# Four graph layers on one core: edge scores taken two slots in a pass, with copies moved between engines and loads respaced

## The chip, the core and the metric

The kernel runs on one core of a Trainium2 chip. The metric is the device time of one execution in microseconds, from the first to the last instruction with what the launch puts around it. The engines are named as in the profile: PE multiplies matrices, DVE is the vector engine, ACT the scalar engine, POOL is GpSimd, which here does nothing but issue indirect (gathering and scattering) DMAs and a few plain ones, and SP issues most of the plain DMAs.

## What is computed

`x` is 16 batches of 1024 nodes with 256 features, `adj` a 1024 x 1024 matrix in which few elements of a row are not zero. All is float32.

```python
# layer 0
pre_u = h @ W1[:d];  pre_v = h @ W1[d:]
hidden = relu(pre_u[:, :, None, :] + pre_v[:, None, :, :] + b1)
S = sigmoid(hidden @ W2 + b2)                       # one score for each pair u, v
a = einsum('buv,bud->bvd', S * adj, h)
m = einsum('uv,bud->bvd', adj, h) * h
z = beta1*h + beta2*(a @ Wa + ba) + beta3*(m @ Wm + bm)
# layer 1
z = z + relu((adj @ z) @ W.T + b)
# layers 2 and 3, with weights of their own
f = z @ W1.T;  f1 = f @ W2 + b2
c = softmax(leaky_relu(f1[:, None] + f1[None, :]) + adj)
z = c @ f + bias2 + z
```

The scores S are needed only where `adj` is not zero, and that is how the kernel takes them.

## The kernel before

**Stages.** Rows of a node are laid on 128 partitions, so there are NT = 8 node tiles. The 16 batches are worked in NGR = 4 groups of GB = 4.

1. *Start* (lines 363 to 505): `load_h` (275) brings the batches of the first group, `load_w1` (151) the weights W1 and Wa. `first_group` turns the features with PE (`turned`) and makes both sides of the edge sum (`edge_sides`, 305), which go to memory as `u_d` and `v_d`. DVE meanwhile finds the non-zero elements of each row of `adj`: up to SLOTS = 32, of which FIRST = 16 belong to the node itself and the others go to XT = 6 tiles of extra rows with QUAD = 4 slots.
2. *First part* (909 to 959): `score_free` does what needs no scores, for all 16 batches: `messages` (332, the product with `adj`), `without_edges` (347), `turned` and `edge_sides` of later groups.
3. *Four groups*, one after another (1302 to 1316). `with_edges` (1058) multiplies the scores of the group, read back from memory (`load_gd`) and reordered by ACT (`gc`, line 1066), with `hw`. Then `pair_layers` (1198) takes two batches at a time through `layer_one` (1134) and the two attention layers: `front` (971) makes the features `f`, `scales` (990) the exponentials `rho` and `tau`, and `sums` (1029) forms for each of 8 node tiles a product `m` on DVE (line 1038) and multiplies it by `f` on PE.

**The scores.** `score_steps` (706) is a generator that runs beside stages 2 and 3, one slot of one node tile in a step, for four batches at once: 128 x 1024 elements. A step gathers the rows of `v_d` for a later slot (`fetch`, 859, by POOL), adds the row of `u` to the gathered rows (807, DVE), takes relu and the product with W2 (809, DVE), and sums each batch's 256 elements with four activations that accumulate (813, ACT). After the last slot of a tile the gates are formed (822 to 829), and their scatters into `dense` are put on a list `waiting`, from which every step issues one or two (788, POOL). A step fetches LEAD = 4 slots ahead, into LEAD + 2 buffers.

**What sets the order.** The order on each engine is fixed when the kernel is built. `Side.along` (869) runs the stage's own generator, which yields its estimated time in us, and takes so many steps of the scores for each of them:

```python
            for us in main:
                self.owed += us * rate
                while self.owed >= 1:
                    self.owed -= 1
                    next(self.steps, None)
```

The rates are RATE = (0.26, 0.255) steps per us. The tool that orders the instructions may put a later instruction of an engine ahead of one that it expects to have to wait. `product` (125) records every matrix product, and `paced` (118) makes an instruction wait for the product that lies `back` = 6 before the latest recorded one, so that side work does not run ahead of PE. One call of `product` becomes two PE instructions.

**Buffers and waits to know.** `sums` has four buffers `m`; `with_edges` has two buffers `gc` and four `gd`; PSUM has eight banks. In `front`, `evacuate` (133) copies a bank by ACT and DVE in turn (lines 138 and 136). `scales` starts `rho` with two DVE instructions out of PSUM (1013). In `with_edges` of the first group, `z_loads` brings four tiles `z` of 1 MB from `zb_d` (at node tiles 2 to 5, line 1073), and then `to_load` brings the transposed `adj` in eight loads, each followed later by an exponential (1076 to 1082). All these, `gd` among them, are issued by SP in order. For the last group there are no scores left: there the third and fourth batch take their neighbours for FAR = 6 node tiles from the lists (`by_lists`, 1139, beside `pair_layers` of the first two batches), which gathers one row of `y_d` at a time, four ahead.

## Time and profile before

| | |
|---|---|
| three timed runs | 3244.6 us median (3230.55 to 3249.76) |
| the profiled execution | 3257.53 us, of it span 3255.8 us |
| granted PE clock, mean | 0.988 |
| busy: PE / DVE / ACT / POOL | 3132.2 / 2433.7 / 1880.1 / 1826.6 us |
| line 807 (DVE, add), line 809 (DVE, relu and product) | 608 of each, 1220 ns each |
| line 813 (ACT, sums) | 2432, 405 ns each, and 188 ns to read the sum |
| line 697 (POOL, gathers of `v_d`) | 512 + 96, 1279 and 1331 ns |
| line 702 (POOL, scatters into `dense`) | 512 + 96, 1238 and 1156 ns |
| lines 136, 138 (copies of features) | 128 at 418 ns (DVE), 128 at 375 ns (ACT) |
| line 1013 (first pass of `rho`) | 64 at 742 ns (DVE) |

A group's mean duration counts from an instruction's start to its end. Instructions of one engine overlap at their edges, so the distance from start to start is shorter: PE's products with 257 columns last 384 ns each in the groups, but 64 of them in a row take 14.0 us. A window of the trace is given as its start and end in us from the start of the span; beside each engine's busy time it lists the number of instructions (x), then the granted PE clock, the share of the DMA engines' time and GB/s. "x <- y" in the waits says that x's engine stood idle until y released it.

### The profile page before, as it was taken

How to read it: one execution, taken by the hardware profiler on the slowest of the kernel's cores; microseconds unless marked ns; L12 is line 12 of the kernel's file. 1: busy time of each engine (PE TensorE's matmuls, PEld its weight loads, DVE VectorE, ACT ScalarE, POOL GpSimd, SP SyncE). 2: the span in 40 equal slices, each digit the busy share in tenths (PEclk: the TensorE clock that was granted, in tenths of full speed). 3: DMA queues.
4: the chain of work that ended last, by engine and by line, in shares of the span. 5: the costliest groups of instructions: out<-in, count | busy, mean ns of one | idle time of the engine just before them, and what ended most of it. 6: DMA issues, size and time to landing. Idle time of an engine off the chain costs nothing. (4 is left out here: it accounts for less than half of the span.)

```text
span 3255.8 us, 39220 instructions
## 1 busy us (share of the span) xinstructions
PE 3132.2 (96%) x12122; PEld 2203.5 (68%) x12122; DVE 2433.7 (75%) x3366; ACT 1880.1 (58%) x6320; POOL 1826.6 (56%) x1483
## 2 busy tenths in 40 slices
PE   8999999999997999999999999999999999999999
PEld 5544544555556678578776867778686678858888
DVE  7787777777775799799668979867898872148754
ACT  3245556566667766566976656688666654413232
POOL 1146888676664666657566666665676550066600
PEclk9999999999998999999999999999999999999999
DMA  8998898879799755656875575587656525475600
GB/s 286 328 323 305 278 288 267 272 226 275 240 322 317 214 162 162 205 154 209 291 226 174 151 221 154 182 286 232 182 151 210 169 90 168 127 246 142 167 15 27
DMA packets 281899, 687.49 MB, mean 211 GB/s; under 512 B 45184, under 2 KB 137344, under 8 KB 274512
## 3 DMA queue, kind: packets, MB, share of 16 engines
q0 software_dynamic: 128224, 387.80, 41.0%
q1 hardware_dynamic: 125472, 245.45, 22.0%
q10 hardware_dynamic: 27984, 51.65, 4.2%
q8 instruction: 97, 1.59, 0.2%
q14 instruction: 122, 1.00, 0.1%
HBM read 553.45 MB, written 131.32 MB: 210 GB/s over the span
## 5 line engine op out<-in xcount | busy, mean ns | idle before, releaser
L813 ACT ACTIVATE z<-z 128x256 f32<-128x256 f32 x2432 | 978.9, 405 | 702.6 <-DVE z L809 613.4
L807 DVE TENSOR_TENSOR z<-z,u 128x1024 f32<-128x1024 f32 x608 | 739.2, 1220 | 402.9 <-PE bank L126 263.0
L126 PE MATMUL bank<-feats,m 128*128 128x257 f32 x4096 | 926.1, 384 | 30.5 <-DVE m L1038 21.7
L697 POOL DMA_INDIRECT z<-v_d,slot_v x512 | 655.1, 1279 | 471.2 <-ACT z L813 241.6
L126 PEld LDWEIGHTS bank<-feats,m 128*128 128x128 f32 x4096 | 768.4, 191 | 160.1 <-DVE m L1038 28.2
L702 POOL DMA_INDIRECT dense_d<-gt,slot_at x512 | 634.1, 1238 | 198.7 <-issue 139.6
L809 DVE SCALAR_TENSOR_TENSOR z<-z,w2r 128x1024 f32<-128x1024 f32 x608 | 737.9, 1220 | 8.5
L126 PE MATMUL bank<-gc,hw 128*128 128x256 f32 x2048 | 459.3, 385 | 33.1 <-ACT gc L1066 28.4
L126 PEld LDWEIGHTS bank<-gc,hw 128*128 128x128 f32 x2048 | 388.4, 192 | 103.4 <-ACT gc L1066 40.5
L813 ACT ACTIVATION_READ_ACCUMULATOR z<-z 128x1 f32 x2432 | 458.2, 188 | 0.0
L126 PE MATMUL bank<-adj_sb,h 128*128 128x512 f32 x1024 | 442.5, 592 | 2.8 <-ACT st L323 2.6
L1038 DVE SCALAR_TENSOR_TENSOR m<-rho,tau,adj_sb 128x512 f32<-128x512 f32 x512 | 374.3, 744 | 69.7 <-PE bank L126 66.2
L126 PE MATMUL bank<-adjT_in,y 128*128 128x512 f32 (+1 forms) x960 | 401.5, 579 | 5.1 <-DMA adjT_in<-adjT_d 2.6
L126 PEld LDWEIGHTS bank<-adj_sb,h 128*128 128x128 f32 x1024 | 194.3, 190 | 243.1 <-issue 237.7
L126 PE MATMUL bank<-w,hT 128*128 128x512 f32 (+1 forms) x1024 | 337.9, 490 | 10.8 <-DMA w<-in_L_gnn_W_dram 8.7
L126 PEld LDWEIGHTS bank<-adjT_in,y 128*128 128x128 f32 x960 | 181.8, 190 | 220.4 <-issue 207.6
L1066 ACT ACTIVATE gc<-gd 128x1024 f32<-128x1024 f32 x128 | 264.6, 2067 | 92.1 <-PE bank L126 53.9
L126 PEld LDWEIGHTS bank<-w,hT 128*128 128x128 f32 x1024 | 195.7, 192 | 154.8 <-issue 131.5
L126 PE MATMUL bank<-g_wT,z 128*128 128x257 f32 x1024 | 235.9, 385 | 1.1 <-DVE z L1117 0.9
L697 POOL DMA_INDIRECT z<-v_d,x_node x96 | 127.7, 1331 | 175.9 <-ACT z L813 108.1
L126 PEld LDWEIGHTS bank<-g_wT,z 128*128 128x128 f32 x1024 | 194.5, 193 | 32.4 <-issue 3.3
L697 POOL DMA_INDIRECT z<-y_d,slot_v x96 | 107.4, 1119 | 62.5 <-DVE msg L1176 41.7
(162 smaller groups left out, 2385.9 us busy)
## 6 DMA issues: line engine op xcount, KB each, us to landing
gd<-dense_d SPq DMA_DIRECT2D x128, 512.0 KB
dense_d<-zero ACTq DMA_DIRECT2D x64, 512.0 KB
adjT_in<-adjT_d SPq DMA_DIRECT2D x112, 256.0 KB
h<-in_x_dram SPq DMA_DIRECT2D x19, 1024.0 KB
u_d<-st SPq DMA_DIRECT2D x64, 256.0 KB
v_d<-st SPq DMA_DIRECT2D x64, 256.0 KB
hw_d<-st SPq DMA_DIRECT2D x64, 256.0 KB
u<-u_d POOLq DMA_DIRECT2D x32, 512.0 KB
```

What stands on the lines that cost most here:

```text
L126: recent.append(nc.tensor.matmul(*args, **kw))
L697: return nc.gpsimd.indirect_dma_start(out=dst, out_offset=None, in_=src[:], in_offset=bass.IndirectOffsetOnAxis(ap=at, axis=0), **how,)
L702: return nc.gpsimd.indirect_dma_start(out=dst[:], out_offset=bass.IndirectOffsetOnAxis(ap=at, axis=0), in_=src, in_offset=None,)
L807: paced(nc.vector.tensor_tensor(z, z, u, ALU.add))
L809: nc.vector.scalar_tensor_tensor(zk, zk, 0.0, w2r[:, None, :].to_broadcast([P, GB, D]), ALU.max, ALU.mult)
L813: nc.scalar.activation(zk[:, c, :], zk[:, c, :], AF.Copy, accum_out=s[:, k, c : c + 1])
L1038: nc.vector.scalar_tensor_tensor(m, r[:, cols], ta[:, jt : jt + 1], ea[:, jt, cols], ALU.max, ALU.mult)
L1066: paced(nc.scalar.activation(gc, gd.rearrange("p n i -> p i n"), AF.Copy), 16)
```

## The change

A step of the scores now takes two slots. The gathered tile is 128 x 2 x 1024 elements, filled by two gathers; line 807 and line 809 each work on all 2048 elements in one instruction (the row of `u` is read twice); the ACT sums stay one for each batch and slot, eight in a step. There are three buffers of two slots, fetched two steps ahead, where there were six of one slot, fetched four ahead. What counts steps is halved: RATE, HOLD, LEAD, the steps of the searches and of the extra rows. A step issues two or three waiting scatters instead of one or two.

Beside that: `front` copies all features by ACT; the first pass of `rho` is an ACT relu with a bias; `by_lists` gathers four rows into one of the same buffers, two buffers ahead; at the start W1 is loaded ahead of the features, whose four pieces all go by SP's queue. In `with_edges` the loads of `z` are spread over every second node tile, with a pace of 12 products, the loads of the transposed `adj` begin with the second quarter (`v` = 1) and their exponentials with the third, and in the first quarter of the first group a node tile counts 1 us and not 3.4 for the rate of the scores. The diff, with some context cut:

```diff
@@ -17,7 +17,7 @@
 BUFS = 2
-RATE = (0.26, 0.255)
+RATE = (0.13, 0.1275)
 SLOTS = 32
@@ -25,9 +25,9 @@
 XT = 6
-HOLD = 40
+HOLD = 20
 FAR = 6
-LEAD = 4
+LEAD = 2
 TOP = 16.0
@@ -272,12 +272,11 @@
-    def load_h(pool, b, pieces=1, other=nc.sync):
+    def load_h(pool, b, pieces=1):
         h = pool.tile([P, NT, D], F32, tag="wide", name="h")
...
         for t in range(0, NT, n):
-            queue = other if t // n % 2 else nc.sync
-            queue.dma_start(h[:, t : t + n, :], x[b, t * P : (t + n) * P].rearrange("(t p) d -> p t d", p=P))
+            nc.sync.dma_start(h[:, t : t + n, :], x[b, t * P : (t + n) * P].rearrange("(t p) d -> p t d", p=P))
         return h
@@ -375,10 +374,9 @@
-        hs = [load_h(early, 0, pieces=4, other=nc.scalar)]
         w1 = load_w1(prep1, nc.scalar)
+        hs = [load_h(early, b, pieces=1 if b else 4) for b in range(2)]
         with_beta2(w1)
-        hs.append(load_h(early, 1))
         for t in range(NT):
@@ -683,7 +681,7 @@
             zs = stack.enter_context(tc.tile_pool(name="zs", bufs=2))
-            slot_pool = stack.enter_context(tc.tile_pool(name="slots", bufs=LEAD + 2))
+            slot_pool = stack.enter_context(tc.tile_pool(name="slots", bufs=LEAD + 1))
             wide_z = stack.enter_context(tc.tile_pool(name="wide_z", bufs=4))
@@ -711,7 +709,7 @@
                 last_of = {g: t for g, t in tiles}
-                todo = [(g, t, k) for g, t in tiles for k in range(FIRST if t < NT else QUAD)]
+                todo = [(g, t, k) for g, t in tiles for k in range(0, FIRST if t < NT else QUAD, 2)]
                 us, zt, ss = {}, {}, {}
@@ -751,7 +749,8 @@
                             fetch(us, zt, *step)
-                    yield
+                    if t % 2:
+                        yield
                 places(own)
@@ -785,18 +784,19 @@
                         last = fetch(us, zt, *todo[n + LEAD])
-                    for _ in range(0 if n < HOLD else 2 if n % 2 and len(waiting) > 4 else 1):
+                    for _ in range(0 if n < HOLD else 3 if len(waiting) > 4 else 2):
                         if waiting:
...
                             after(tc, ins, [last], later, "behind the gather")
-                    if moving:
-                        group, *what = moving.pop(0)
-                        ins = scatter(*what)
-                        group.add(ins)
-                        after(tc, ins, [last], later, "behind the gather")
-                        arrive = n + 12
+                    for _ in range(2):
+                        if moving:
+                            group, *what = moving.pop(0)
+                            ins = scatter(*what)
+                            group.add(ins)
+                            after(tc, ins, [last], later, "behind the gather")
+                            arrive = n + 6
                     slots, _, at, av = lists(t)
@@ -804,20 +804,23 @@
                         sources(us, *follows[g, t])
-                    paced(nc.vector.tensor_tensor(z, z, u, ALU.add))
-                    zk = z.rearrange("p (c k) -> p c k", k=D)
+                    u2 = u[:, None, :].to_broadcast([P, 2, GB * D])
+                    paced(nc.vector.tensor_tensor(z, z, u2, ALU.add))
+                    zk = z.rearrange("p s (c k) -> p (s c) k", k=D)
                     nc.vector.scalar_tensor_tensor(
-                        zk, zk, 0.0, w2r[:, None, :].to_broadcast([P, GB, D]), ALU.max, ALU.mult
-                    )
-                    for c in range(GB):
-                        nc.scalar.activation(zk[:, c, :], zk[:, c, :], AF.Copy, accum_out=s[:, k, c : c + 1])
+                        zk, zk, 0.0, w2r[:, None, :].to_broadcast([P, 2 * GB, D]), ALU.max, ALU.mult
+                    )
+                    for c in range(2 * GB):
+                        nc.scalar.activation(
+                            zk[:, c, :], zk[:, c, :], AF.Copy, accum_out=s[:, k + c // GB, c % GB : c % GB + 1]
+                        )
                     if n < NT:
...
                         places(others)
-                    if n == NT + 4:
+                    if n == NT + 2:
                         moved = to_extra_rows()
-                    if k == slots - 1:
+                    if k == slots - 2:
                         sv = s[:, :slots, :].rearrange("p s c -> p (s c)")
@@ -836,7 +839,7 @@
                         got = from_extra_rows(moved)
-                    if got is not None and n == arrive + 24:
+                    if got is not None and n == arrive + 12:
                         unpack(got)
@@ -857,8 +860,10 @@
             def fetch(us, zt, g, t, k):
-                z = zt[g, t, k] = slot_pool.tile([P, GB * D], F32, tag="z", name="z")
-                return gather(z, v_d[g], lists(t)[1][:, k : k + 1])
+                z = zt[g, t, k] = slot_pool.tile([P, 2, GB * D], F32, tag="z", name="z")
+                for i in range(2):
+                    last = gather(z[:, i, :], v_d[g], lists(t)[1][:, k + i : k + i + 1])
+                return last
@@ -979,7 +984,7 @@
                         )
-                    evacuate(f[:, jt, :], ps[:, : D + 1])
+                    nc.scalar.activation(f[:, jt, :], ps[:, : D + 1], AF.Copy)
                     if jt == 1:
@@ -1010,7 +1015,7 @@
                 for v in range(NV):
-                    nc.vector.tensor_scalar(r[:, v * HN : (v + 1) * HN], banks[v], sh[:, 3:4], 0.0, ALU.add, ALU.max)
+                    nc.scalar.activation(r[:, v * HN : (v + 1) * HN], banks[v], AF.Relu, bias=sh[:, 3:4])
                 nc.vector.tensor_scalar(sh[:, 1:2], sh[:, 0:1], -0.01, None, ALU.mult)
@@ -1070,17 +1075,17 @@
                                 )
-                        if z_loads and ut > 1:
+                        if z_loads and ut % 2 == 0:
                             load, i = z_loads.pop(0)
-                            paced(load(i))
-                        if (to_load or to_exp) and ut % 2 and not z_loads:
-                            if v and to_exp:
+                            paced(load(i), 12)
+                        if (to_load or to_exp) and ut % 2 and v:
+                            if v > 1 and to_exp:
                                 exponential(to_exp.pop(0))
...
                                 to_exp.append(jt)
-                        yield 3.4
+                        yield 3.4 if g or v else 1
                     if v == N // QN - 1:
@@ -1151,34 +1156,40 @@
                 todo += [(t, FIRST + q) for t in range(FAR) for q in range(NG)]
-                got = {}
-
-                def fetch_row(t, k):
-                    z = got[t, k] = slot_pool.tile([P, GB * D], F32, tag="z", name="z")[:, : 2 * D]
-                    if t < NT and k >= FIRST:
-                        at = (k - FIRST) * NT + t
-                        gather(z, part_d, to_u[:, at : at + 1])
-                    else:
-                        gather(z, y_d, lists(t)[1][:, k : k + 1])
-
-                for step in todo[:LEAD]:
-                    fetch_row(*step)
-                for n, (t, k) in enumerate(todo):
-                    if n + LEAD < len(todo):
-                        fetch_row(*todo[n + LEAD])
-                    z = got.pop((t, k))
-                    to = msg[t] if t < NT else part[t % len(part)]
-                    if t < NT and k >= FIRST:
-                        paced(nc.vector.tensor_tensor(to, to, z, ALU.add))
-                    elif k == 0:
-                        paced(nc.vector.tensor_scalar(to, z, lists(t)[3][:, k : k + 1], None, ALU.mult))
-                    else:
-                        paced(nc.vector.scalar_tensor_tensor(
-                            to, z, lists(t)[3][:, k : k + 1], to, ALU.mult, ALU.add
-                        ))
-                    if t >= NT and k == QUAD - 1:
-                        nc.sync.dma_start(part_d[(t - NT) * P : (t - NT + 1) * P, :], to)
-                    yield
+
+                fours = [todo[i : i + 4] for i in range(0, len(todo), 4)]
+                got = []
+
+                def fetch_rows(some):
+                    z = slot_pool.tile([P, 2, GB * D], F32, tag="z", name="z").rearrange("p a (b n) -> p (a b) n", b=2)
+                    for i, (t, k) in enumerate(some):
+                        if t < NT and k >= FIRST:
+                            at = (k - FIRST) * NT + t
+                            gather(z[:, i, :], part_d, to_u[:, at : at + 1])
+                        else:
+                            gather(z[:, i, :], y_d, lists(t)[1][:, k : k + 1])
+                    got.append(z)
+
+                for some in fours[:LEAD]:
+                    fetch_rows(some)
+                for n, some in enumerate(fours):
+                    if n + LEAD < len(fours):
+                        fetch_rows(fours[n + LEAD])
+                    zs4 = got.pop(0)
+                    for i, (t, k) in enumerate(some):
+                        z = zs4[:, i, :]
+                        to = msg[t] if t < NT else part[t % len(part)]
+                        if t < NT and k >= FIRST:
+                            paced(nc.vector.tensor_tensor(to, to, z, ALU.add))
+                        elif k == 0:
+                            paced(nc.vector.tensor_scalar(to, z, lists(t)[3][:, k : k + 1], None, ALU.mult))
+                        else:
+                            paced(nc.vector.scalar_tensor_tensor(
+                                to, z, lists(t)[3][:, k : k + 1], to, ALU.mult, ALU.add
+                            ))
+                        if t >= NT and k == QUAD - 1:
+                            nc.sync.dma_start(part_d[(t - NT) * P : (t - NT + 1) * P, :], to)
+                        yield
```

## The prediction

> **What bounds the kernel.** I read the page, then windows of 100 us, the groups by shape, the waits and the timeline of the stretches that stood out.
>
> ```profile
> PE 3132.2 (96%) x12122; PEld 2203.5 (68%) x12122; DVE 2433.7 (75%) x3366; ACT 1880.1 (58%) x6320; POOL 1826.6 (56%) x1483
> ```
>
> PE is the bound, and all that can be won is what it stands idle: 3255.8 - 3132.2 = 124 us, and some of the 1.2% of clock that idling costs. Where, the windows tell (busy PE, PEld, DVE, ACT, POOL):
>
> ```profile
> 400.00:500.00 100.00, 98.33 (x275) 48.93 (x274) 72.05 (x75) 54.95 (x234) 80.81 (x66) 1.00 0.88 282
> 900.00:1000.00 100.00, 85.19 (x264) 51.78 (x263) 56.90 (x59) 60.01 (x201) 59.76 (x50) 0.91 0.91 323
> 1200.00:1300.00 100.00, 97.00 (x469) 82.63 (x468) 98.61 (x150) 66.59 (x250) 61.69 (x46) 1.00 0.57 162
> 1157.00:1501.00 344.00, 331.91 (x1442) 256.60 (x1441) 310.58 (x452) 219.79 (x834) 220.03 (x168) 1.00 0.58 168
> 1734.00:2101.00 367.00, 353.68 (x1537) 274.54 (x1537) 331.97 (x485) 237.92 (x895) 230.25 (x175) 0.99 0.58 169
> 2311.00:2698.00 387.00, 370.89 (x1605) 288.63 (x1604) 331.69 (x493) 235.27 (x874) 232.75 (x178) 0.99 0.53 157
> ```
>
> In the first part (400) PE is full, with POOL the next: 80.8 us in 66 issues, and as an issue follows the last by 0.30, it has no idle time at all (80.8 + 66 x 0.30 = 100.6). Between first part and groups (900) PE loses 15 us and clock. In the three attention stretches PE is idle 41.6 us of 1098 and DVE busy 974; there DVE is the second bound, as the timeline shows:
>
> ```profile
> 1242.27 0.75 DVE L1038 SCALAR_TENSOR_TENSOR m<-rho,tau,adj_sb 128x512 f32<-128x512 f32 x1
> 1242.93 1.22 DVE L807 TENSOR_TENSOR z<-z,u 128x1024 f32<-128x1024 f32 x1
> 1244.07 0.75 DVE L1038 SCALAR_TENSOR_TENSOR m<-rho,tau,adj_sb 128x512 f32<-128x512 f32 x1
> ```
>
> Start to start, m takes 0.66 and a pass 1.14, 1.80 together, with no gap, where PE needs 8 x 0.217 = 1.74 for one m. So a DVE that has less to do lets PE run.
>
> **The change, part by part.** The sum is made in the profiled execution, 3257.5 us, and set off from the median of the runs, 3244.6, which is 12.9 lower.
>
> ```profile
> L807 DVE TENSOR_TENSOR z<-z,u 128x1024 f32<-128x1024 f32 x608 | 739.2, 1220 | 402.9 <-PE bank L126 263.0
> L136 DVE COPY feats<-bank 128x257 f32<-128x257 f32 x128 | 53.0, 418 | 12.8 <-PE bank L126 11.9 <-issue 0.5
> L138 ACT ACTIVATE feats<-bank 128x257 f32<-128x257 f32 x128 | 46.5, 375 | 61.2 <-PE bank L126 54.4 <-issue 4.7 <-PE bank L1004 1.8
> L1013 DVE TENSOR_SCALAR rho<-bank,shift 128x512 f32<-128x512 f32 x64 | 44.9, 742 | 0.0
> L1116 ACT ACTIVATE r<-bank,l1b 128x512 f32<-128x512 f32 x60 | 38.3, 678 | 71.2 <-PE bank L126 39.8 <-DVE msg L1176 26.4 <-DMA out_dram<-st 4.9
> ```
>
> 1. *DVE's relief in attention: -36.* A two-slot pass: the 512-wide addition of line 1117 takes 686, the 1024-wide 1220, so 1.043 ns an element; 2048 take 2.29 us, 2.20 in a stream, for two of 1.14. The 249 slots of the three stretches save 249 x 0.07 = 17 us. Three of four groups have scores: 96 copies (0.34 in a stream) and 48 passes of rho (0.66) leave DVE, 32 + 32. Together 81 of 974 us. DVE is over 90% busy in 6 of the 11 windows of 100 us, so 44 count; PE's idle time caps it at 41.6; I take off 5 for ACT, whose sums now come as eight in a row (8 x 0.40 = 3.2 us, not 1.6) ahead of what ends a `sums`. ACT gains 96 x 0.375 + 48 x 0.68 = 69 us in stretches where it is busy 693 of 1098, so the moved work is covered. Bounds: -41.6; and +70, if m runs out: a pass starts at the earliest when PE has five products left, 5 x 0.43 = 2.17 us, and the next m is there after 2.20 + 0.74 = 2.94; 0.77 in each of some 91 pairs that fall into `sums`. Four buffers of m, three of them ready (5.2 us), speak against that.
>
> The page "ScalarE: Activation LUTs", Rules for kernel authors, says to give relu, add and copies to VectorE, since it is up to about 3 times faster; that is for bf16. If it held here, ACT would get 3 x 64 x 0.742 = 142 us for rho. The rows above say 678 against 742 ns, and 375 against 418, and they decide.
>
> 2. *POOL beside longer passes: +15.* What a POOL issue takes depends on DVE:
>
> ```profile
> 1560.94 1.23 DVE L809 SCALAR_TENSOR_TENSOR z<-z,w2r 128x1024 f32<-128x1024 f32 x1
> 1561.62 1.40 POOL L697 DMA_INDIRECT z<-v_d,slot_v  x1 [2.10 <-ACT z L813]
> 1568.34 1.23 DVE L807 TENSOR_TENSOR z<-z,u 128x1024 f32<-128x1024 f32 x1 [1.10 <-PE bank L126]
> 1568.53 1.89 POOL L697 DMA_INDIRECT z<-v_d,slot_v  x1 [0.30 <-issue]
> ```
>
> Both issues end 0.85 after the pass beside which they started (1562.17 + 0.85 = 1563.02; 1569.57 + 0.85 = 1570.42); alone one takes 0.97, 1.27 with its gap. So an issue waits for the pass to end. In 350 to 550 POOL is full: 66 x 0.97 = 64.0 of 80.8 us, so 16.8 us per 100 are such waits, for some 53 passes. If an issue starts at an even chance in a pass of 1.14 this would be 53 x 0.89 x (0.57 - 0.12) = 21; the trace has 0.8 of it. A pass of 2.20 always catches one, in its first 1.27 us: (2.20 - 0.64 - 0.12) x 0.8 = 1.15, 26 times in 100 us, 30 us. That is +13 per 100 us for 250 full us, 33. A late gather first eats the time in which line 807 waits for its pace (71 us from 200 to 950, so 24 in this third): +9 is left, +15 with the burst of extra rows, which now falls later, onto the first scatters (20 to 26 steps in). Queued behind a late gather: line 807, then on DVE mT and zb, for which PE waits in `without_edges`. Bounds: 0 if what an issue waits for does not grow with the pass (no pass of the trace is longer than 1.23 us); +60 if three full windows lose 20 each and nothing is eaten. I take the side near the line that the two issues lie on.
>
> The page "SBUF — State Buffer", Who interferes with whom, says that a DVE instruction with two SBUF inputs holds a port shared with GpSimd for the whole instruction; by it an issue in a longer pass waits to its end (+15); if the port were given back inside one, it would not (0). This rule speaks against longer passes.
>
> 3. *Between the parts: -16.*
>
> ```profile
> PE bank L126 <- ACT gc L1066: 19.0, 8, 14.3
> ACT gc L1066 <- DMA gd<-dense_d: 13.0, 2, 12.8
> ```
>
> These are the waits of 930 to 1100. SP issues four z of 1 MB from 964.9 to 976.5, and the gd behind them lets PE stand for 14.3 us. Now one z goes out every second node tile (6.9 us), and the eight loads of adj come later, eight tiles further. Of the 19.0 I take the 14.3 and 2 of the rest. The eight exponentials (8.3 us of ACT) move one quarter on and cost there what they cost now. Bounds: 0 to -19.
>
> 4. *gc beside eight sums: +8.* A node tile of `with_edges` is 16 x 0.216 = 3.45 us of PE and 2.07 of ACT. Two tiles with one pair: 2 x 2.07 + 3.2 = 7.34 for 6.9, so 0.44 and more for each of 36 pairs, 16; the present waits of this kind outside part 3 are 28.4 - 19.0 = 9.4, so +7, +8 as some bursts lie worse. Bounds -9 and +56 (a burst that starts just before gc: 1.8 each).
>
> 5. *Start: -6.*
>
> ```profile
> PE bank L126 <- DMA w<-in_L_gnn_W_dram: 8.7, 1, 8.7
> ```
>
> W1 is now issued first. Bounds: -9.3 (with 0.6 for Wa); +4.5, the time PE waits for h now, if h takes twice as long on one queue.
>
> 6. *End of the scores: +3.* The first quarter gives (3.4 - 1) x 8 x 0.1275 = 2.4 pairs less; the scores end some 19 us later. Now the last scatter is issued at 2683.9 and PE starts on that group at 2717.7; landing, gd and gc need some 12. Bounds 0 and +15.
>
> 7. *Lists: -6.*
>
> ```profile
> 3095.50 1.09 PE L1193 MATMUL bank<-ident,msg 128*128 128x128 f32 x4 [5.48 <-issue]
> ```
>
> PE stood 3.5 and 5.5 us for the last rows, which POOL issued one each 1.26 us; with 8 to 12 rows ahead and not 4 to 6, four or five are there already. Bounds -10, +2. Halved counters, searches and pool size cost nothing; DVE's searches are the same.
>
> Sum: -36 + 15 - 16 + 8 - 6 + 3 - 6 = -38, so 3219.5 for the profiled execution and **3207** against the median.
>
> **Rivals.** *Slower: POOL becomes the bound.* Per pair POOL needs 4.1 issues x 1.27 = 5.2, 0.5 behind the m's, and twice the wait for a pass. A pair lasts 1098 / 125 = 8.78 us in attention, 8.46 with part 1; it decides from (8.46 - 5.7) / 2 = 1.38 a wait. I have 1.15, and 1.44 without the factor 0.8, so it is near. At 1.65 a pair takes 9.0: +28 there; (26 x 1.65 - 16.8) x 2.5 - 24 = +41 in the first part; the other parts -17: 3297. For it: POOL without idle time in the first part. Against: 21% idle in attention. *Slower: m runs out*, part 1 at +70: 3313. *DVE's time is not on the path:* part 1 at 0 and part 3 at half: 3251. For it: PE is busy 97% there already. *Faster:* nothing held longer, all idle time won: -42 + 0 - 19 - 9 - 9 + 0 - 10 = -89: 3156.
>
> **How the numbers follow.** Forecast 0.38 (its own range 3180 to 3235, three quarters of it below 3212); faster rival 0.18; not on the path 0.19; POOL 0.18; m runs out 0.07. About 1% is what a measurement of this kernel can tell from no change. Faster: 0.28 + 0.18 = 0.46; same: 0.10 + 0.19 = 0.29; slower 0.25. The range 3150 to 3300 leaves out half of POOL's case, m's, and a little below: 0.19.
>
> **What would show it.** Right: L807 near 2290 ns x304; DVE below 94% in 1200 to 1300; no wait of 10 us for gc near 980. POOL's issues near 1.6 us mean and line 807 waiting longer on "DMA z<-v_d" confirm part 2; over 1.7, with PE idle from 350 to 700, POOL's rival. Idle PE with "DVE m L1038" growing from 21.7 us shows m running out. The sum is wrong if attention's 41.6 us do not shrink.

## The result, and the profile after

The changed kernel takes 3481.5 us (median of 6 runs, 3477.5 to 3487.7) against 3242.7 of the kernel before (6 runs): ratio 1.0749, 95% interval 1.0727 to 1.0770. It is slower by 239 us where 38 less were predicted. Its profiled execution took 3487.7 us, span 3486.0. Kernels' times below are medians, and one execution of e9, at 6677 us twice as long as the other three, is left out of its row. "Before" and "after" name the kernel before and the changed one, a pair is the two slots of a step, and the weight pass is line 809 (810 after), relu and product with `w2`.

The page's line of engines, after:

```profile
PE 3198.5 (92%) x12122; PEld 2231.4 (64%) x12122; DVE 2295.1 (66%) x2566; ACT 1930.6 (55%) x6512; POOL 2199.8 (63%) x1483
```

DVE was relieved as planned, 2433.7 to 2295.1. POOL went the other way with the same 1483 instructions, 1826.6 to 2199.8: 373 us more. PE's span grew by 230, of which 66 are PE being "busy" longer with the same 12122 products (more on this at the end) and 164 are idle.

Windows of the kernel before (first fence) and after (second): the middle of the first part and three stretches of attention in which both have the same products (PE's counts agree within 4), and after also one window. Columns as in the prediction: PE, PEld, DVE, ACT, POOL, clock, DMA share, GB/s.

```profile
300.00:850.00 550.00, 546.71 (x1538) 278.04 (x1537) 411.19 (x435) 325.17 (x1358) 415.32 (x334) 1.00 0.84 263
...
1179.00:1555.00 376.00, 361.74 (x1601) 284.59 (x1600) 340.23 (x499) 241.99 (x909) 239.51 (x181) 1.00 0.61 178
1757.00:2132.00 375.00, 361.65 (x1596) 284.09 (x1596) 342.17 (x502) 241.78 (x907) 239.28 (x179) 0.99 0.60 175
2341.00:2717.00 376.00, 361.79 (x1593) 286.71 (x1594) 315.08 (x475) 223.55 (x818) 222.20 (x169) 0.99 0.52 152
```

```profile
300.00:850.00 550.00, 485.45 (x1292) 241.99 (x1291) 328.67 (x241) 268.54 (x1130) 456.05 (x302) 0.93 0.73 226
...
1200.00:1300.00 100.00, 93.78 (x303) 57.17 (x302) 65.06 (x58) 61.53 (x242) 75.56 (x50) 0.97 0.57 169
...
1293.00:1700.00 407.00, 371.28 (x1600) 291.45 (x1601) 315.27 (x367) 251.23 (x950) 280.24 (x181) 0.96 0.54 165
1919.00:2322.00 403.00, 366.43 (x1598) 289.07 (x1599) 319.50 (x374) 252.80 (x949) 296.22 (x185) 0.97 0.55 169
2543.00:2934.00 391.00, 367.52 (x1589) 290.70 (x1589) 304.50 (x367) 237.61 (x898) 283.84 (x178) 0.97 0.50 153
```

With its gaps of 0.30, POOL has 456.05 + 302 x 0.30 = 547 of 550 us in the first part: full for all of it. Before it had 415.32 + 334 x 0.30 = 516, so 34 us to spare, and PE stood for 3.3; now PE stands for 64.6. In attention no engine is full: DVE 78% where it had 89, POOL 72% without its gaps (62 before), and PE idles 95.8 us of 1201 where it had 41.8 of 1127.

Groups of the changed kernel (engine, operation, busy, mean ns | idle before, and what ended it):

```profile
L808 DVE TENSOR_TENSOR z<-z,u 128x2048 f32<-128x2048 f32 x304 | 696.2, 2290 | 660.9 <-DMA z<-v_d,slot_v 300.5
L695 POOL DMA_INDIRECT z<-v_d,slot_v x512 | 846.4, 1653 | 395.4 <-ACT z L814 230.8
L700 POOL DMA_INDIRECT dense_d<-gt,slot_at x512 | 751.0, 1467 | 179.3 <-issue 148.3
```

The addition takes the 2290 ns that were forecast. Gathers went from 1279 to 1653 ns, scatters from 1238 to 1467; over all 1216 issues of gathers of `v_d` and scatters the mean is 1.558 us, forecast "near 1.6" (before 1.256). The waits of after, for the lines of before (total us, times, longest):

```profile
DVE z L808 <- DMA z<-v_d,slot_v: 300.5, 73, 15.4
DVE z L808 <- PE bank L126: 225.1, 89, 19.5
...
PE bank L126 <- DVE m L1043: 53.5, 18, 14.2
...
PE bank L126 <- ACT gc L1071: 45.0, 37, 6.1
...
PE bank L126 <- ACT st L322: 40.5, 10, 8.7
...
PE bank L126 <- DVE mT L342: 38.3, 10, 14.6
```

Before, DVE waited 63.9 us for gathers, 31 times; now 300.5. What stands behind the waiting addition in DVE's queue can be late with it, and these waits grew: PE's for `m` (21.7 before) and `mT` (4.5), and for ACT's `st` (2.6) and `gc` (28.4). One such wait in the timeline of after:

```profile
421.00 2.29 DVE L810 SCALAR_TENSOR_TENSOR z<-z,w2r 128x2048 f32<-128x2048 f32 x1
421.58 2.56 POOL L695 DMA_INDIRECT z<-v_d,slot_v  x1 [0.30 <-issue]
424.44 0.96 POOL L695 DMA_INDIRECT z<-v_d,slot_v  x1 [0.30 <-issue]
425.70 1.01 POOL L700 DMA_INDIRECT dense_d<-gt,slot_at  x1 [0.30 <-issue]
...
431.45 2.29 DVE L808 TENSOR_TENSOR z<-z,u 128x2048 f32<-128x2048 f32 x1 [8.16 <-DMA z<-v_d,slot_v]
```

The first gather of a pair is held by the weight pass until 424.14, 0.85 after that pass (421.00 + 2.29). The second follows at once and takes 0.96, as DVE is idle; its rows are there 6.05 us after it ends, and DVE has stood for 8.16 us. In the groups POOL is not full, but its scatters can come in a row ahead of the gather that DVE needs next:

```profile
1529.61 0.97 POOL L700 DMA_INDIRECT dense_d<-gt,slot_at  x1 [0.31 <-issue]
...
1549.30 0.97 POOL L700 DMA_INDIRECT dense_d<-gt,slot_at  x1 [0.30 <-issue]
1550.57 0.98 POOL L695 DMA_INDIRECT z<-v_d,slot_v  x1 [0.30 <-issue]
...
1557.20 2.29 DVE L808 TENSOR_TENSOR z<-z,u 128x2048 f32<-128x2048 f32 x1 [13.48 <-DMA z<-v_d,slot_v]
```

From 1529.61 to 1550.27 it issues thirteen scatters and nothing else.

### The profile page after: what moved, and what is told of

It reads as the page before. It is cut to its first block, busy times and chain, and to the rows that moved or that the text cites. A ratio compares the mean times of both kernels' runs of the same rounds, so it can differ in the third digit from the quotient of the medians.

```text
span 3486.0 us, 38260 instructions
## 1 busy us (share of the span) xinstructions
PE 3198.5 (92%) x12122; PEld 2231.4 (64%) x12122; DVE 2295.1 (66%) x2566; ACT 1930.6 (55%) x6512; POOL 2199.8 (63%) x1483
## 5 line engine op out<-in xcount | busy, mean ns | idle before, releaser
L808 DVE TENSOR_TENSOR z<-z,u 128x2048 f32<-128x2048 f32 x304 | 696.2, 2290 | 660.9 <-DMA z<-v_d,slot_v 300.5
L695 POOL DMA_INDIRECT z<-v_d,slot_v x512 | 846.4, 1653 | 395.4 <-ACT z L814 230.8
L126 PE MATMUL bank<-feats,m 128*128 128x257 f32 x4096 | 933.6, 386 | 61.5 <-DVE m L1043 53.5
L126 PEld LDWEIGHTS bank<-feats,m 128*128 128x128 f32 x4096 | 777.7, 193 | 184.3 <-DVE m L1043 42.1
L700 POOL DMA_INDIRECT dense_d<-gt,slot_at x512 | 751.0, 1467 | 179.3 <-issue 148.3
L810 DVE SCALAR_TENSOR_TENSOR z<-z,w2r 128x2048 f32<-128x2048 f32 x304 | 695.0, 2286 | 5.0
L126 PE MATMUL bank<-adj_sb,h 128*128 128x512 f32 x1024 | 451.3, 602 | 22.5 <-ACT st L322 22.5
L126 PE MATMUL bank<-w,hT 128*128 128x512 f32 (+1 forms) x1024 | 349.6, 502 | 25.4 <-ACT st L322 18.0
L1071 ACT ACTIVATE gc<-gd 128x1024 f32<-128x1024 f32 x128 | 261.9, 2064 | 121.5 <-PE bank L126 72.1
L126 PE MATMUL bank<-g_wT,z 128*128 128x257 f32 x1024 | 247.5, 397 | 23.1 <-DVE z L1122 14.9
L695 POOL DMA_INDIRECT z<-v_d,x_node x96 | 152.9, 1593 | 140.8 <-ACT z L814 104.3
L700 POOL DMA_INDIRECT dense_d<-gt,x_at x96 | 144.5, 1505 | 29.3 <-issue 28.0
```

The source lines that it names most:

```text
L126: recent.append(nc.tensor.matmul(*args, **kw))
L695: return nc.gpsimd.indirect_dma_start(out=dst, out_offset=None, in_=src[:], in_offset=bass.IndirectOffsetOnAxis(ap=at, axis=0), **how,)
L700: return nc.gpsimd.indirect_dma_start(out=dst[:], out_offset=bass.IndirectOffsetOnAxis(ap=at, axis=0), in_=src, in_offset=None,)
L808: paced(nc.vector.tensor_tensor(z, z, u2, ALU.add))
L810: nc.vector.scalar_tensor_tensor(zk, zk, 0.0, w2r[:, None, :].to_broadcast([P, 2 * GB, D]), ALU.max, ALU.mult)
L1071: paced(nc.scalar.activation(gc, gd.rearrange("p n i -> p i n"), AF.Copy), 16)
```

## The experiments

The runs are e1 to e20, without an e4 and an e14. Runs on one chip share a letter: A has e1, e2, e3, e6; B has e5, e7, e8, e9, e13, e15, e16; C has e10, e11, e12; D has e17 to e20. One kernel's ratio differed by 1% between two chips (e16 and e20), so differences are taken on one chip where there are such. The kernel before took 3240.7 on A, 3243.8 and 3244.4 on B, 3227.3 on C and 3226.2 on D; e6, e7, e8 and e10 have two executions each. "First part" is the time at which `with_edges` first starts, then follow the lengths of the three groups with scores and of the rest, all from the traces (the profiled execution of before was 15 us above its median, that of after 6); "issue" is the mean of POOL's 1216 gathers of `v_d` and scatters into `dense`.

| kernel | us | ratio to before, 95% | issue us | first part, groups, rest |
|---|---|---|---|---|
| before | 3242.7 | | 1.256 | 956, 593, 584, 585, 538 |
| after | 3481.5 | 1.0727 to 1.0770 | 1.558 | 1064, 632, 626, 620, 544 |
| e1 passes cut (A) | 3741.5 | 1.1539 to 1.1609 | 1.167 | 1177, 667, 685, 657, 543 |
| e2 pairs only (A) | 3497.1 | 1.0777 to 1.0832 | 1.550 | 1068, 643, 625, 621, 544 |
| e3 other edits only (A) | 3225.4 | 0.9939 to 0.9972 | 1.243 | 953, 580, 578, 573, 540 |
| e6 half the scatters (A) | 3342.7 | 1.0291 to 1.0370 | 1.606 (of 912) | 998, 606, 601, 593, 549 |
| e5 cut, in order (B) | 3349.6 | 1.0291 to 1.0362 | 1.370 | 983, 610, 599, 602, 544 |
| e7 fourth buffer (B) | 3468.2 | 1.0622 to 1.0743 | 1.549 | 1045, 627, 624, 615, 543 |
| e8 w2 in PSUM (B) | 3422.5 | 1.0498 to 1.0585 | 1.473 | 1006, 628, 625, 615, 549 |
| e9 e3, four buffers (B) | 3294.5 | 1.0114 to 1.0202 | 1.252 | 985, 609, 577, 576, 546 |
| e13 slot by slot (B) | 3317.9 | 1.0186 to 1.0251 | 1.219 | 982, 603, 599, 585, 546 |
| e15 late sums (B) | 3319.5 | 1.0196 to 1.0259 | 1.197 | 989, 603, 599, 588, 542 |
| e16 e11 + fours (B) | 3251.9 | 1.0013 to 1.0044 | 1.217 | 977, 579, 578, 582, 541 |
| e10 e5 + fourth (C) | 3327.5 | 1.0280 to 1.0332 | 1.373 | 985, 609, 601, 597, 534 |
| e12 e5, six single (C) | 3324.0 | 1.0278 to 1.0322 | 1.362 | 989, 606, 602, 592, 530 |
| e11 e3 + w2 in PSUM (C) | 3206.7 | 0.9915 to 0.9948 | 1.218 | 952, 574, 574, 567, 538 |
| e17 e13, single rows (D) | 3253.5 | 1.0057 to 1.0097 | 1.206 | 970, 580, 588, 579, 536 |
| e18 e3, pair steps (D) | 3312.8 | 1.0251 to 1.0286 | 1.349 | 972, 603, 601, 589, 537 |
| e19 e11 again (D) | 3208.3 | 0.9932 to 0.9961 | 1.215 | 952, 574, 574, 569, 537 |
| e20 e16 again (D) | 3202.4 | 0.9908 to 0.9938 | 1.218 | 952, 579, 574, 568, 530 |

In the expectations "ring" means the buffers that the gathers fill in turn, and "coarse steps" that the work of two slots is handed over at once, half as often.

**Which edits? e2 and e3.** e3 is the kernel before with these edits of the change, and nothing of the pairs:

```diff
-                    evacuate(f[:, jt, :], ps[:, : D + 1])
+                    nc.scalar.activation(f[:, jt, :], ps[:, : D + 1], AF.Copy)
-                    nc.vector.tensor_scalar(r[:, v * HN : (v + 1) * HN], banks[v], sh[:, 3:4], 0.0, ALU.add, ALU.max)
+                    nc.scalar.activation(r[:, v * HN : (v + 1) * HN], banks[v], AF.Relu, bias=sh[:, 3:4])
...
-                        if z_loads and ut > 1:
+                        if z_loads and ut % 2 == 0:
```

> Kernel before (one slot in a pass, six buffers), with only the edits beside the passes: copies of features and rho's first pass on ScalarE, the part change spread, W1 ahead of the features of the graphs. Theory: these are not what was lost, and a part of the predicted relief is seen: 3190 to 3235. Rival, the edits beside the scores cost the time: over 3300.

e2 is the other half, the changed kernel with these edits undone.

> Changed kernel, with the edits beside the passes taken back: copies of features alternate between VectorE and ScalarE, rho's first pass is on VectorE, the part change loads and the start are as before. Theory, the length of the pass: the loss stays, and what the edits beside it may bring is lost too, 3480 to 3540. Rival, the edits beside the scores cost the time: about 3245.

Measured on one chip, before 3240.7: e3 -15 us, e2 +256. Together +241, and the change has +239: the pairs of slots cost it all, and the other edits gain a little, by the traces in the groups.

**GpSimd? e6.** Half of the scores stay out of `dense`:

```diff
-                        for j in range(slots):
+                        for j in range(0, slots, 2):
```

> Changed kernel that leaves out every second scatter of scores, so half of the scores never reach the dense matrix; passes, gathers, buffers and sums stay. Theory, GpSimd is the bound in the first part and late in bursts after it: with a quarter of its issues gone the gathers come in time, 3330 or less, and line 808 waits for its gathers well under 300 us. Rival, the coarse steps or the eight sums in a row: 3450 or more, since nothing there changes. If it is GpSimd and only the length of the pass lies behind it, this and the cut passes both win.

3342.7, 12.7 above what the theory gave, but 139 below the change, and 154 below e2 on the same chip (some 15 of it are the other edits, which e2 lacks). Of the 154 the first part has 70 and the three groups 89; the rest is 5 longer. Passes, gathers and buffers are those of the change; only POOL, and the DMA queue behind it, have less to do, and DVE's wait for gathers falls from 300.5 us to this:

```profile
DVE z L808 <- DMA z<-v_d,slot_v: 129.8, 45, 10.2
```

**The length of the pass? e1, then e5.** e1 cuts each instruction of 2048 elements in two:

```diff
-                    paced(nc.vector.tensor_tensor(z, z, u2, ALU.add))
+                    for i in range(2):
+                        ins = nc.vector.tensor_tensor(z[:, i, :], z[:, i, :], u, ALU.add)
+                        if i == 0:
+                            paced(ins)
```

(and line 810 in the same way.)

> Changed kernel, with each two-slot instruction of VectorE cut into two of one slot (128x1024); three buffers of two slots, eight sums in a row and all the rest stay. Theory, the length of the pass: a GpSimd issue waits for the end of the VectorE pass beside it, so its mean for the gathers of v_d and the scatters falls from 1.56 us back to about 1.26 (the kernel before) and the time to 3190 to 3260. Rival, the coarse steps: three buffers of two slots let a gather start later and in pairs; then the issues get shorter but the time stays above 3400. Rival, the edits beside the scores: the time stays above 3400 as well. In between, both have a share.

Issues fell to 1.167 us, and the time rose to 3741.5. By its words the rival of the coarse steps has it (shorter issues, above 3400), but neither foresaw a time 260 us above the change's. The tool that orders the instructions now drew the four short ones apart. From the first addition to the end of the last weight pass, a buffer of two slots was held 9.4 us from 300 to 850, where the change has 4.8, and POOL waited for buffers, not for DVE's passes:

```profile
POOL z L695 <- ACT z L818: 929.4, 166, 21.8
...
DVE z L809 <- DMA z<-v_d,slot_v: 591.2, 151, 19.2
```

So e1 changed two things. e5 keeps the order of the change (each of the four instructions behind the one before):

```diff
+                    for one, then in zip(cut, cut[1:]):
+                        after(tc, then, [one], later, "in this order")
```

> As e1, but the four one-slot instructions of a pair keep the order of the two long ones (add, add, weight, weight), so a buffer is held by VectorE for about 5 us again and not for the 9 of e1. Theory POOL (an issue waits for the end of a long pass, and GpSimd is full): issues back to 1.17 to 1.27 us, with_edges starts before 990 instead of at 1064, time 3230 to 3330. Theory ring (three buffers of two slots come free too late, whatever an issue takes): issues short as well, but start after 1040 and time above 3420.

The first part, 983, is as the theory says; issues, 1.370, and time, 3349.6, lie between theory and change. The time is 119 less than that of e7 (below) on the same chip, which has the long passes and a buffer more. The length of the pass is about half of the loss, 62 us of it before `with_edges` first starts.

**What holds the issue? e8.** `w2` is copied to a PSUM bank for the first part (seven banks are left to the products there):

```diff
+                w2p = held.tile([P, HN], F32, name="w2p")
+                nc.scalar.activation(w2p[:, :D], w2r, AF.Copy)
+                psum_pool(first, "banks1", 7)
...
+                    w2 = w2p[:, :D] if n < 100 else w2r
```

> Changed kernel with w2 in a PSUM bank during the first part (seven banks left to the products there), so the pass of line 810 reads one operand from SBUF and one from PSUM there; its length stays. Theory: what holds a GpSimd issue is a VectorE instruction with two inputs from SBUF, so issues beside this pass take 0.97 to 1.0 us, the mean of the first part's issues falls by 0.2 to 0.3 us and with_edges starts at 970 to 1030. Rival: any long pass holds an issue, then nothing changes: start 1050 to 1080.

First part 1006 instead of 1064 in the change (and 1045 in e7, on the same chip), with one bank less. The timeline of e8:

```profile
443.01 2.29 DVE L807 TENSOR_TENSOR z<-z,u 128x2048 f32<-128x2048 f32 x1 [4.00 <-DMA z<-v_d,slot_v]
443.45 2.69 POOL L694 DMA_INDIRECT z<-v_d,slot_v  x1 [0.30 <-issue]
445.34 2.29 DVE L810 SCALAR_TENSOR_TENSOR z<-z,w2p 128x2048 f32<-128x2048 f32 x1
446.45 1.02 POOL L699 DMA_INDIRECT dense_d<-gt,slot_at  x1 [0.30 <-issue]
```

Both passes take 2.29. Beside the addition (two inputs from SBUF) the issue takes 2.69 and ends 0.84 after the pass; beside the weight pass with one input from PSUM it takes 1.02 and ends inside it. 101 issues that start beside such a pass have a mean of 0.98 us, while the 89 beside additions have 2.32. So the length alone does not hold an issue: the second input from SBUF does. Nor is it the kind of instruction: later in e8, with `w2` back in SBUF, 171 issues that start beside the same pass have 2.22, and 32 beside `mT`, a TENSOR_TENSOR that reads a bank, 0.98. The Trainium skill, page "SBUF — State Buffer", Who interferes with whom, says that a VectorE instruction with at most one SBUF input, outside its two-port fast modes, does not contend with GpSimd. The 0.98 us of e8 agree.

**The buffers? e7, e9, e10, e12.** e7 gives the first part a fourth buffer of two slots, e10 the same to e5, e12 gives e5 six buffers of one slot, and e9 takes two of six from e3 and gathers three slots ahead, not four.

```diff
+                fourth = pool.tile([P, 2, GB * D], F32, name="fourth")
...
+                    if n < FOURTH:
+                        f = n + LEAD + 1
+                        last = fetch(us, zt, *todo[f], fourth if f % 4 == 3 else None)
```

> Changed kernel with a fourth buffer of two slots in the first part alone (gathers three pairs ahead until pair 96; the tiles of gc are allocated behind the first part to make room). Two-slot passes stay. Theory ring: the first part falls from 944 us back to 850 to 880 (with_edges starts at 970 to 1000), time about 3400. Theory POOL: issues stay at 1.5 us or more, GpSimd stays full from 300 to 850, with_edges still starts after 1035, time above 3450.

> e3 (one slot in a pass) with four buffers of one slot and gathers three slots ahead instead of six and four. Theory ring: the buffers matter by themselves, 3330 or more, with issues at 1.2 to 1.25 us and GpSimd waiting for ScalarE's sums. Theory POOL alone: issues as in e3, 3260 or less.

> e5 (cut passes in order) with the fourth buffer of e7 in the first part. With short passes GpSimd has a little time to spare there, so if the coarse ring holds the rest of the first part, with_edges starts at 955 to 968 instead of 983 (e3 has 953). If GpSimd's issues hold it still (1.365 us in the first part of e5, 1.21 in e3, 406 of them: 63 us more), the start stays at 976 to 988.

> e5 with six buffers of one slot in place of three of two: the four short instructions of a pair still run add, add, weight, weight, gathers are still issued in pairs and sums eight in a row, but a slot's buffer is free after its own four sums. Theory ring: most of the 125 us by which e5 is above e3 goes, 3230 to 3280. Rival, the coarse steps (back to back passes that leave GpSimd no gap, issues in pairs): 3310 to 3350, issues still 1.35 us or more.

e7's first part is 1045, 19 below the change, as the theory of POOL has it: a full POOL hardly issues earlier for a buffer more. e10 and e12 start at 985 and 989 where e5 has 983, both runs as expected if the buffers do not matter, and their ratios lie in e5's interval. So the buffers by pairs are not what is left. e9 falls between its two ranges and shows that four single ones would be too few: 43 us above e16 on its chip, of which some 11 are e16's `w2` in PSUM and lists (ratios of e3 and e20, 0.9956 and 0.9923).

**The rest: e13, e15, e18, e17.** e12 has the pass length, the pass count and the buffers of e3, and its ratio is still 3.4% above (1.0300 and 0.9956). What is left is the coarse step and what it groups: the passes of a pair stand as a block (two additions, two weight passes), and gathers, scatters and sums come for two slots. e13 puts e12's passes in the order addition, weight, addition, weight, with a slot's four sums behind each; e15 is e13 with the eight sums in a row.

> e12 (six buffers of one slot) with the four short instructions of a pair in the order add, weight, add, weight and a slot's four sums right behind its weight pass, as in e3; what is left of the change is that gathers, scatters and the pace come once in two slots. If the blocks (two additions, then two weight passes, then eight sums) hold the 98 us by which e12 is above e3: 3225 to 3265. If the coarse step holds them: 3300 to 3330.

> e13 with the eight sums of a pair in a row behind its second weight pass. If it is ScalarE's burst that costs time within the blocks, this is above e13 by 30 us or more; if VectorE's order, or the coarse step, it is within 15 us of e13.

e15 equals e13: eight sums in a row cost nothing. e13, in the range of the coarse step, seemed to say that the blocks cost little, but its chip, B, is the one on which e16 lost 1%. e18 comes from the other side: e3 with the coarse step alone.

```diff
-RATE = (0.26, 0.255)
+RATE = (0.13, 0.1275)
...
-                    yield
+                    if n % 2:
+                        yield
```

> e3 (one slot in a pass, six buffers, gathers, scatters and sums by slot) with one thing of the change: two slots are put into the streams at once, half as often (rates halved, a step ends after every second slot). If the coarse step costs the 92 us between e13 and e3, 3290 to 3320; if it is the grouping of gathers and scatters on GpSimd's queue, 3220 to 3245.

> e13 with the lists of the last layer by single rows, as before the change. If the fours of rows cost what separates e16 from e11 (45 us), wherever it arises: about 3275. If they cost nothing by themselves: 3305 to 3325.

e18 is at 3312.8, 104 above e19 on its chip (3 to 8 of it are e19's `w2` in PSUM, by the ratios of e3, e11 and e19). Nothing in it is longer or larger than in e3; two steps are handed to the tool at once, half as often. Groups of e18:

```profile
L806 DVE TENSOR_TENSOR z<-z,u 128x1024 f32<-128x1024 f32 x608 | 725.8, 1220 | 464.0 <-PE bank L126 233.7 <-DMA z<-v_d,slot_v 110.7 <-issue 69.2
...
L700 POOL DMA_INDIRECT dense_d<-gt,slot_at x512 | 683.0, 1334 | 192.1 <-issue 125.8 <-DVE gt L825 35.1 <-DMA dense_d<-gt,slot_at 11.1
L695 POOL DMA_INDIRECT z<-v_d,slot_v x512 | 670.2, 1309 | 463.1 <-ACT z L812 241.0 <-issue 77.7 <-DVE m L1038 37.8
```

The passes take 1220 ns as before, but the issues are longer, and DVE waits 110.7 us for gathers (59.7 in e3). The order shows why: on DVE the tool sets the two additions of a step side by side 229 times in e18, 45 times in e3. In 199 of 304 steps the four passes then run as a block with nothing between them (45 times in e3), and so without an instruction that reads PSUM, beside which POOL could issue in 0.98 us. Issues that start beside a weight pass have a median of 1.95 us in e18, 1.09 in the first part of e3 and 1.20 later. (An `m` is no such instruction; it reads two operands from SBUF, and the 105 issues that start beside one in after have a mean of 1.31 us.) e17 forces addition, weight, addition, weight (6 side by side) in the same coarse step: issues 1.206 us, and 59 us less than e18 on the same chip, its groups nearly as short as e3's; that is below both ranges that were expected of it. e13 has this order too. Of the 1.4% between its ratio and e17's, the old lists of e17 cannot be much (e19 and e20), and the two chips alone made 1.05% between e16 and e20.

**A faster version: e11, e16, e19, e20.** e11 is e3 with `w2` in PSUM in the first part; e16 adds the lists in fours. e19 and e20 are these two again, side by side.

> e3 (one slot in a pass, edits beside the scores) with w2 in a PSUM bank during the first part. By e8 the 102 issues that stand beside the weight pass there (1.40 us mean in e3) fall to 0.98: 43 us of GpSimd, of which it needs back what falls into the 250 us in which it is full. 3200 to 3222, issues of the first part at about 1.10 us. Rival: seven banks instead of eight cost PE more than that, 3228 or more.

> e11 (the fastest so far) with the lists of the last layer gathered four rows to two buffers, as the change does it. From the last start of with_edges to the end e11 takes 537 us, e12 530, so 3 to 8 us less than e11's 0.9931 of before: 0.9905 to 0.993. Rival: the lists do not matter, 0.993 to 0.995.

> e11 once more, on the chip of the other three runs, so that they are compared on one chip: 0.990 to 0.996 of before. If it is above 1.0 here, what e16 lost lies with the chip and not with the lists.

> e16 once more, beside e11 on one chip. If the lists cost it, 30 to 50 us above e19; if it was the chip, within 10 us of e19.

e11 is faster than before and after on both chips where it ran, 0.9915 to 0.9948 and 0.9932 to 0.9961; that is 0.5 to 0.7%, less than what B and D differ by, and it did not run on B. The fours take another 6 us on D (e20), but the same kernel was 0.3% slower than before on B (e16), so it can't be called the better one.

## Why the prediction was wrong

The steps by their numbers:

1. *DVE's relief, -36: wrong in the changed kernel.* DVE fell by 139 us in all, and from 89 to 78% of the attention stretches. But PE's idle time there, predicted to fall from 41.6 by 36, is 95.8: DVE has time and no rows. The edits that do not touch the passes (copies, `rho`, part 3 and the start) gain 15 us alone (e3); 28 of the 36, the 16 and the 6 were counted for them, 50. The mechanism is there (in the three stretches with the same products PE idles 41.8 us before and 21.6 in e3's trace), and the time shows a third of the size.
2. *POOL beside longer passes, +15: the price was right, the amount was the main failure.* An issue that starts in a pass still ends 0.84 us (median) after it when the pass takes 2.29, and the mean issue came out as said: (1.558 - 0.97) x 1216 / 608 = 1.18 us of wait a pass, forecast 1.15. It failed at "+13 per 100 us for 250 full us", less 24 for the pace, and at leaving attention out. From 300 to 850 POOL had 34 us to spare in 550. It had 334 issues for 145 slots there, 4.6 a pair and not the 4.1 of the rival's working, for the scatters of the early tiles wait in a list. At the measured 1.51 + 0.30 that is 4.6 x 1.81 = 8.3 us a pair, where a pair had 550 / 72.5 = 7.6: the sum from the row should have been about 55 us here alone (334 x 1.81 = 605 in 550). Measured are 108 us to the first `with_edges`; e8 and e5 give back 58 and 81 of them (39 and 62 against e7, on their own chip) by shortening only what an issue waits for. The pace did not eat it: DVE's wait for PE fell by 38 us, its wait for gathers rose by 237. In the groups, POOL's mean load hid that DVE's next gather stands behind scatters (the timeline at 1557); from e7 to e5 the three groups lose 55 us, and half the scatters take 89 off them (e2 and e6).
3. *Between the parts, -16: the wait is gone in e3.* Its window from 900 to 1000 and the wait for `gc` (28.4 us, longest 14.3, before) show it:

```profile
900.00:1000.00 100.00, 95.55 (x335) 63.03 (x334) 56.42 (x62) 66.12 (x186) 52.25 (x46) 1.00 0.94 328
```

```profile
PE bank L126 <- ACT gc L1064: 19.3, 13, 3.7
```

   PE has 10 us more in the window, where 16 were counted; what that is worth in e3's time is not separated from its other edits. In the changed kernel late rows cover it.
4. *gc beside eight sums, +8: size wrong, and the reason.* Waits for `gc` are 45.0 against e3's 19.3, +26. Eight sums in a row are not why: e13 has 33.3 and e15 34.4, so 14 come with the coarse step, whatever the sums' order. The other 12 come with the late rows; that these make ACT late is likely, not shown.
5. *Start, -6:* the wait of 8.7 us for W1 is gone, PE waits 8.4 for `h` instead of 4.5, and the first product with `adj` starts 3 us earlier (120.0 for 122.8). In the other kernels with the new start it begins at 118.6 to 122.2, and in e2, with the old one, at 121.5, so a gain is not shown.
6. *End of the scores, +3:* the rest after the last start of `with_edges` is 544 against 538; no run separates it.
7. *Lists, -6:* e20 is 6 us below e19, with intervals that overlap. That agrees, no more.

And one sentence of the prediction put a term at nothing and gave no reason: "Halved counters, searches and pool size cost nothing." The pool size does cost next to nothing. The halved counters cost about 100 us (e18), some 59 of them through the order that two steps at once get (e17). So the 256 us of the pairs are: length of the passes beside POOL about 120 (e7 to e5), the coarse step about 100 (e18 against e3 by ratio, two chips), and some 35 that stay open. These are read on different kernels and do not add up exactly: by ratios the change is 4.2% or 137 us above e5, which would leave some 20; e7 has a fourth buffer that the change has not. And e17, without blocks and long passes, still has 45 us over e19 on its chip (3 to 8 of it e19's `w2` in PSUM). Whether the coarse step by itself or gathers and scatters that come in groups cost these was not tried.

The rival "POOL becomes the bound" was the right one, with 0.18 for it and 3297 us. Its point of decision, 1.38 us of wait a pass, was worked out from attention; the first part had (7.6 - 4.6 x 1.27) / 2 = 0.9, and 1.15 had been predicted. Worked by stage, it would have been on this rival's side. Its number was still 185 us short: it had 41 us for the first part, which lost 108, and nothing for the coarse step. "m runs out" seems to be in it as a consequence: that wait rose from 21.7 to 53.5 us.

## What to carry to other kernels

Before lengthening an instruction, look up who waits for it on other engines, and count their issues stage by stage: a queue that is 70% busy on average, gaps included, was 94% busy for 550 us, and 108 of the 230 us that the trace grew by had been lost by the end of that first part. A counter that is only halved is an edit too: two steps handed over at once come out in another order, here on DVE, so try it alone, with nothing else changed. Where a long VectorE pass runs beside GpSimd's DMA issues, put one of its inputs into PSUM: in e8, with the long passes, this took 58 us off the first part. With the short ones a gain is not shown: issues of the first part fell from 1.21 to 1.11 us, but it ended at 952 instead of 953 (e3, e11, e19), and the intervals of the ratios overlap.

## What the runs showed of the hardware

- The hold is one-sided. 139 issues in the trace of after were under way up to 0.9 us before a long pass began; their median is 0.97 to 1.00 us whatever the distance, and the 89 of them that began with VectorE idle took at most 1.03. So an issue waits only at its start; nine took 3.1 to 3.6 us, all begun beside another VectorE instruction, seven of them beside an `m`. And the passes keep their time: 2266 to 2311 ns from the 1st to the 99th percentile. The Trainium skill, page "SBUF — State Buffer", SBUF: two separate sides, says that whichever starts first keeps the port pair for its whole instruction and the other blocks. These 139 passes started beside an issue under way and were not blocked.
- PE's idle time is paid twice. Busy time times granted clock is the same for the 12122 products, 3132.2 x 0.988 = 3095 before and 3198.5 x 0.967 = 3093 after (3062 to 3104 in all twenty traces): with 164 us more idleness came 66 us of slower products. The idleness comes first: in the trace of after PE stands for over 3 us 27 times (9 before), and after 25 of these (all 9) the clock is recorded at 0.50 when PE resumes or within 12 us.
- One kernel can differ between chips. e16 and e20 are one kernel, on B and on D: 3251.9 and 3202.4, while before had 3244.4 and 3226.2 beside them, ratios 1.0028 and 0.9923. Their instructions come in the same order as e11's until the last group, yet the first part ended at 977 and 952. e11 and e19, also one kernel, agree on C and D (0.9931 and 0.9946). An interval from one chip can be narrower than what another chip gives.
